# A state-space scan's 128x128 products split into 64x64 products on quadrants of the array

## The chip, the cores and the metric

The kernel runs on one core of a Trainium2 chip. The metric is device time in microseconds (us), from the launch to the end of one execution; smaller is better. A core has a matrix engine (TensorE, PE in the profile, with its weight loads as PEld), a vector engine (VectorE, DVE), an engine for activations (ScalarE, ACT), a general engine (GpSimd, POOL) and one that issues transfers (SyncE, SP). Each runs its own queue in order and waits for the others through semaphores. Matrix products are written to PSUM, a small memory of banks; everything else lives in SBUF, 128 partitions wide.

## The reference

The program is a Perceiver of two layers. 16 batches of 64 latent tokens of width 128 (1,024 tokens, `X`) attend to 1,601 context tokens per batch with 16 heads; each layer adds the attention, then a sequence model, then a feed-forward. The second layer's sequence model is a state-space scan with four heads of width 64 and state 64:

```python
dt = softplus(x @ dt_w.T + dt_b)
Bm = (x @ B_w.T).reshape(B_, L, NHEADS, D_STATE)
Cm = (x @ C_w.T).reshape(B_, L, NHEADS, D_STATE)
A = -exp(A_log)
def step(h, inp):
    x_t, dt_t, B_t, C_t = inp
    A_bar = exp(A[None, :] * dt_t)[..., None, None]
    h = A_bar * h + dt_t[..., None, None] * B_t[:, :, None, :] * x_t[..., None]
    y_t = einsum('bhpn,bhn->bhp', h, C_t) + D[None, :, None] * x_t
    return h, y_t
```

The scan starts from zero for each batch and runs over its 64 tokens. Written without a loop, y at token t is the sum over tokens s up to t of (C_t . B_s) times exp of the sum of A dt over the tokens after s up to t, times dt_s x_s, plus D x_t. That is a 64x64 lower-triangular matrix per batch and head. No token of one batch touches another batch.

## The kernel before

The attention is one long stream of steps. A step n of a group (a batch and half of its heads, `step`) issues one scores matmul of 512 columns (line 697, tile `s`) and, about 21 steps later, four averages of 129 columns (line 760, tile `av`). ScalarE evicts the scores (line 710) and takes their exponential (line 748); VectorE keeps the running maximum (line 705) and subtracts it (line 747). Three PSUM banks hold scores, two hold averages, and three more, with the tag `tp`, are shared by all other products.

Everything else is fed into this stream. `run` holds a list of generators, `between`, for the sequence models and feed-forwards of finished token groups. At each step it has a budget; the generator of the first entry is advanced, and the number that it yields, a guess at VectorE's work, is taken off the budget. A yielded tuple instead postpones the next advance by so many steps. The instructions that come out are then placed by a planner with estimates of its own, under order constraints set by `behind`, so neighbouring instructions can change places. For the second layer the entries are, in turn, `scan1` and `ffn` for chunks 0-1, 2-3, 4-5, then 6, then 7 (a chunk, c, is 128 tokens: two batches). The last entries, for chunk 7, run after the attention has ended, with nothing beside them but dummy products (`fill`, line 130).

In `scan1` a chunk goes through these products, each over both batches of the chunk at once, 128 tokens by 128 tokens:

- Line 1272 (`af`): on VectorE, the mask `after` (token later than another, same batch) times A dt, for four heads, 128x512.
- Line 1299 (`gr`): B transposed times C, per head, with 64 rows (the state) by 128 tokens, 128 columns. Two PSUM banks per chunk, one for each half of the state rows. Line 1301 (`gm`) copies it to SBUF times the mask `upto`.
- Line 1307 (`seg`): `af` times `upto`, per head, gives the sums of A dt in the exponent; line 1310 takes the exponential back into `af`.
- Line 1320: `gm` times `af`.
- Line 1326 (`sy`): the result times dt x (`xd`, line 1286 on GpSimd), 128 rows by 128 tokens, 64 columns per head; line 1329 adds it to D x.

The two masks are zero wherever the tokens are of different batches; they are made by GpSimd in `setup_rest`, lines 274 to 287. For the last chunk the exponential and the product after it are done in two halves of the heads (`parts`, line 1267).

Of the kernel before, what the change touches and what calls it, by code (L numbers as in the profile page):

```python
# [36 lines left out]
AF = mybir.ActivationFunctionType  # L37
ALU = mybir.AluOpType
# [4 lines left out]
P = 128  # L43
NB, L, D = 16, 64, 128
# [29 lines left out]
CG = 2  # L74
# [5 lines left out]
class Kernel:  # L80
# [171 lines left out]
    def setup_rest(self):  # L252

        nc, a, tc = self.nc, self.a, self.tc
        self.col = self.cst([P, 44], "col")
        nc.sync.dma_start(out=self.col, in_=a["col128"])

        self.ycol = self.cst([P, 4], "ycol")
        nc.sync.dma_start(out=self.ycol, in_=a["vec256"].rearrange("(n p) -> p n", p=P))
        nc.vector.tensor_scalar_mul(self.ycol, self.ycol, 0.5)  # L260

        self.half = self.cst([P, 10], "half")
        nc.vector.tensor_scalar_mul(self.half, self.col[:, C_CW:C_CW + 10], 0.5)
        self.vecs = self.cst([P, 20], "vecs")
        nc.sync.dma_start(out=self.vecs, in_=a["vecs"].partition_broadcast(P))

        self.na0, self.na1 = self.cst([P, 2, NS], "na0"), self.cst([P, 4], "na1")
        nc.scalar.activation(self.na0, self.col[:, C_ALOG:C_ALOG + 2 * NS].rearrange("p (k s) -> p k s", k=2), AF.Exp)
        nc.vector.tensor_scalar(self.na0, self.na0, 1e-6, 1.0, ALU.max, ALU.min)
        nc.vector.tensor_scalar_mul(self.na0, self.na0, -1.0)  # L270
        nc.scalar.activation(self.na1, self.vecs[:, V_AL:V_AL + 4], AF.Exp)
        nc.vector.tensor_scalar_mul(self.na1, self.na1, -1.0)

        self.upto = self.cst([P, P], "upto")
        nc.gpsimd.memset(self.upto, 1.0)
        nc.gpsimd.affine_select(
            out=self.upto, in_=self.upto, compare_op=ALU.is_ge, fill=0.0, base=0,
            pattern=[[1, P]], channel_multiplier=-1,
        )
        nc.gpsimd.memset(self.upto[0:64, 64:128], 0.0)  # L280
        self.after = self.cst([P, P], "after")
        nc.gpsimd.memset(self.after, 1.0)
        nc.gpsimd.affine_select(
            out=self.after, in_=self.after, compare_op=ALU.is_gt, fill=0.0, base=0,
            pattern=[[-1, P]], channel_multiplier=1,
        )
        nc.gpsimd.memset(self.after[64:128, 0:64], 0.0)
        iota_i = self.cst([P, NE], "iota_i", I32)
        nc.gpsimd.iota(iota_i, pattern=[[1, NE]], base=0, channel_multiplier=0)
        self.iota = self.cst([P, NE], "iota")  # L290
        nc.vector.tensor_copy(self.iota, iota_i)
        self.iota8 = self.cst([P, NE], "iota8")
        nc.vector.tensor_scalar_add(self.iota8, self.iota, float(NE))
        yield 1.0

        self.mcol = self.cst([P, G + 1, NB], "mcol")
        with tc.tile_pool(name="msk", bufs=1) as one:
            m8 = one.tile([NB, S], U8, tag="m8", name="m8")
            nc.sync.dma_start(out=m8, in_=a["mask"])
            mf = one.tile([NB, S], F32, tag="mf", name="mf")  # L300
            nc.vector.tensor_scalar(mf, m8, -1.0, -NEG, ALU.add, ALU.mult)
            t = self.tp("mskT")
            for g in range(G + 1):
                n = P if g < G else REM
                nc.tensor.transpose(t[:n, g * NB:(g + 1) * NB], mf[:, g * P:g * P + n], self.ident[:NB, :NB])
            me = t[:, (G + 1) * NB:(G + 2) * NB]
            nc.tensor.transpose(me, mf[:, SK:SK + 1].to_broadcast([NB, P]), self.ident[:NB, :NB])
            nc.vector.tensor_copy(self.mcol[:, :G, :].rearrange("p g b -> p (g b)"), t[:, :G * NB])
            nc.vector.tensor_copy(self.mcol[:REM, G, :], t[:REM, G * NB:(G + 1) * NB])
            nc.vector.memset(self.mcol[REM:, G, :], 0.0)  # L310
            self.mex = self.cst([P, NB], "mex")
            nc.vector.tensor_copy(self.mex, me)
        yield 2.0
        yield from self.quant_weights()
# [843 lines left out]
    def scan1(self, c0, CG):  # L1158
        nc, tc, a = self.nc, self.tc, self.a
        X = self.X[:, c0:c0 + CG, :]  # L1160
        TG, BG = CG * P, 2 * CG
        NH, HD = 4, 64
        last = c0 + CG == C and CG == 1
        with tc.tile_pool(name="sd1", bufs=1) as one, tc.tile_pool(name="sd2", bufs=CG) as work:
# [24 lines left out]
            if last:  # L1189
                cv = self.tp("cv")  # L1190
                for k in range(2):
                    o = cv[:, k * TG:(k + 1) * TG]
                    nc.tensor.matmul(o, self.wcb[:, k * P:(k + 1) * P], self.one, start=(k == 0), stop=False)
                for k in range(2):
                    o = cv[:, k * TG:(k + 1) * TG]
                    for i in range(4):
                        mm = nc.tensor.matmul(o, self.wcv[k][:, i, :], padded[:, :, i:i + L], start=False, stop=(k == 1 and i == 3))  # L1197
                self.fill(3, mm)
            else:
                t = self.tp("xz")  # L1200
# [6 lines left out]
                for k in range(2):  # L1207
                    o = cv[:, k * TG:(k + 1) * TG].rearrange("p (b l) -> p b l", l=L)
# [11 lines left out]
            t = self.tp("sdt")  # L1220
# [13 lines left out]
            t = self.tp("sz")  # L1234
# [19 lines left out]
            def bc(dst, m):  # L1254
                t = self.tp("sb")
                for hh in range(2):
                    for k in range(2):
                        nc.tensor.matmul(t[:, hh * TG:(hh + 1) * TG], m[:, k, hh * P:(hh + 1) * P], xc[:, k, :], start=(k == 0), stop=(k == 1))
                nc.scalar.copy(dst.rearrange("p h t -> p (h t)"), t[:, :2 * TG])

            bT, cT = t1([P, 2, TG], "bT"), t1([P, 2, TG], "cT")
# [2 lines left out]
            yield HOP1  # L1264
            nc.vector.scalar_tensor_tensor(dt, dt, 0.0, ln, ALU.max, ALU.add)
            nc.vector.tensor_tensor(adt, dt, self.row(self.na1, shape), ALU.mult)
            parts = ((0, 2), (2, NH)) if last else ((0, NH),)

            full = [P, NH, P]
            af = [work.tile(full, F32, tag="af", name=f"af{c}") for c in range(CG)]  # L1270
            for c in range(CG):
                x = nc.vector.tensor_tensor(af[c], self.row(self.after, full), self.bc(adt[:, c, :], full), ALU.mult)
            if last:
                self.later(nc.vector.scalar_tensor_tensor(*silu), x)
            bc(cT, CwT)
            yield 0.6 + 0.7 * CG

            xr, xd = t1([P, CG, NH, HD], "xr"), t1([P, CG, NH, HD], "xd")
            t = self.tp("sx")
# [11 lines left out]

            gm = [work.tile(full, F32, tag="gm", name=f"gm{c}") for c in range(CG)]
            for c in range(CG):
                tok = slice(c * P, (c + 1) * P)
                for i in range(2):
                    g = self.tp(f"gr{c}{i}")
                    part = slice(i * HD, (i + 1) * HD)
                    for k in range(2):
                        nc.tensor.matmul(g[:, k * P:(k + 1) * P], bT[part, k, tok], cT[part, k, tok], start=True, stop=True)
                    gi = gm[c].rearrange("p (k i) t -> p i k t", i=2)[:, i]  # L1300
                    nc.vector.tensor_tensor(gi, g[:, :2 * P].rearrange("p (k t) -> p k t", k=2), self.row(self.upto, [P, 2, P]), ALU.mult)
                yield 0.9
            for c in range(CG):
                for lo, hi in parts:
                    sg = self.tp(f"seg{c}")
                    for h in range(lo, hi):
                        mm = nc.tensor.matmul(sg[:, h * P:(h + 1) * P], af[c][:, h, :], self.upto, start=True, stop=True)  # L1307
                    if last and hi == NH:
                        self.fill(2, mm)
                    decay = nc.scalar.activation(af[c][:, lo:hi, :].rearrange("p h t -> p (h t)"), sg[:, lo * P:hi * P], AF.Exp)  # L1310
                yield 0.1
            for dst, i in ((zb, 2), (z, 0)):
                for k in range(2):
# [2 lines left out]
                        self.later(x, decay)  # L1316
            yield HOP1
            for c in range(CG):
                for lo, hi in parts:
                    nc.vector.tensor_tensor(gm[c][:, lo:hi, :], gm[c][:, lo:hi, :], af[c][:, lo:hi, :], ALU.mult)  # L1320
                yield 0.8
            yield HOP
            for c in range(CG):
                o = self.tp(f"sy{c}")
                for h in range(NH):
                    mm = nc.tensor.matmul(o[:, h * HD:(h + 1) * HD], gm[c][:, h, :], xd[:, c, h, :], start=True, stop=True)
                if last:
                    self.fill(5, mm)
                nc.vector.tensor_tensor(y[:, c, :], y[:, c, :], o[:, :256], ALU.add)
                yield 0.4  # L1330
# [3 lines left out]
            t = self.tp("syt")  # L1334
            for c in range(CG):
                for k in range(2):
                    mm = nc.tensor.transpose(t[:, k * TG + c * P:k * TG + (c + 1) * P], y[:, c, k * P:(k + 1) * P], self.ident)
# [3 lines left out]
            t = t[:, :2 * TG]  # L1341
# [372 lines left out]
```

## Time and profile before

| | |
|---|---|
| Median of 3 runs | 1975.37 us (1974.5 to 1977.61) |
| Profiled execution | 1973.36 us |
| Its span, first to last instruction | 1971.6 us |
| TensorE busy | 1931.2 us |
| VectorE busy | 1582.9 us |
| ScalarE busy | 1383.5 us |
| GpSimd busy | 512.3 us |
| Mean granted TensorE clock | 0.998 of full speed |

The products `gr`, `seg` and `sy` of the five scans lie at 1498 to 1512 us of the span, 1602 to 1625, 1777 to 1789, 1892 to 1899 and 1946 to 1950. Up to about 1934 the attention runs beside them.

A line of the profile names an engine, the source line, the operation, the tile written and the tiles read, a size in partitions by elements, and a count. In order of time the first two numbers are start and length in us; what stands in square brackets is how long the engine was idle before, and who ended it. Matmuls are pipelined, so the length of one includes its way through the array: the pace of a stream is read from one start to the next. The operations of float32 matmuls are recorded as two instructions each.

### The profile page before, as it was taken

Reading aid. Unit: us, or ns where it says so; the run is one execution under the profiler, and the core shown is the slowest. Engines: PE = TensorE matmul, PEld = TensorE weight load, DVE = VectorE, ACT = ScalarE, POOL = GpSimd, SP = SyncE. Lnnn points to the kernel's source line nnn. Section 1 sums busy time; section 2 is a strip of 40 time slices with the busy share of each in tenths; the row PEclk is TensorE's granted clock in tenths of the full one; section 3 lists DMA queues with packets and bytes.
Section 4 is the critical chain, followed back from the end, with each engine's and each line's share of the span. In section 5 each row is a group of like instructions: output and inputs, shape, how many; then the busy total and the mean of one; then the engine's idle time right before and its main releaser. Section 6 shows DMA issues by size and latency. Waiting matters only on the chain. (4 is left out here: it accounts for less than half of the span.)

```text
span 1971.6 us, 32642 instructions
## 1 busy us (share of the span) xinstructions
PE 1931.2 (98%) x11987; PEld 1478.8 (75%) x11987; DVE 1582.9 (80%) x3029; ACT 1383.5 (70%) x2638; POOL 512.3 (26%) x579
## 2 busy tenths in 40 slices
PE   8999999999999999999999999999999999999998
PEld 5777777677777767777777777777778777787786
DVE  6977776987878887876998878898786978778875
ACT  5888787887868878666776657776665665766651
POOL 5211122543123452121452202542110111101000
PEclk9999999999999999999999999999999999999999
DMA  6121112322122221221221112221120210201000
GB/s 184 46 68 51 39 54 77 85 67 70 35 76 85 66 77 53 67 78 59 77 82 54 41 40 64 70 58 54 49 67 1 58 37 19 59 18 37 23 1 23
DMA packets 146223, 111.86 MB, mean 57 GB/s; under 512 B 13827, under 2 KB 132367, under 8 KB 146063
## 3 DMA queue, kind: packets, MB, share of 16 engines
q1 hardware_dynamic: 145518, 109.51, 19.1%
q8 instruction: 95, 1.56, 0.3%
q14 instruction: 66, 0.53, 0.1%
q10 hardware_dynamic: 544, 0.26, 0.0%
HBM read 81.28 MB, written 27.41 MB: 55 GB/s over the span
## 5 line engine op out<-in xcount | busy, mean ns | idle before, releaser
L760 PEld LDWEIGHTS av<-kv,st 128*128 128x128 f32 x6656 | 870.0, 192 | 376.6 <-issue 357.5
L760 PE MATMUL av<-kv,st 128*128 128x129 f32 x6656 | 881.8, 275 | 4.0 <-DVE aq L769 4.0
L697 PE MATMUL s<-qT,kvT 128*128 128x512 f32 x1664 | 859.3, 599 | 7.4 <-ACT st L712 5.5
L748 ACT ACTIVATE st<-st 128x1024 f32<-128x1024 f32 (+1 forms) x448 | 444.3, 996 | 120.7 <-DVE st L747 114.1
L747 DVE TENSOR_TENSOR st<-st,mb 128x1024 f32<-128x1024 f32 (+1 forms) x448 | 503.7, 1134 | 17.9 <-PE mb L739 17.9
L710 ACT ACTIVATE st<-s,mcol 128x512 f32<-128x512 f32 x416 | 283.2, 684 | 191.3 <-DVE R L705 167.6
L712 ACT COPY st<-s 128x512 f32<-128x512 f32 x416 | 240.0, 580 | 133.6 <-DVE R L707 121.4
L705 DVE SCALAR_TENSOR_TENSOR R<-s,mcol,R 128x512 f32<-128x512 f32 x352 | 262.2, 745 | 43.9 <-PE s L697 42.4
L707 DVE TENSOR_TENSOR R<-s,R 128x512 f32<-128x512 f32 x352 | 241.0, 685 | 61.9 <-PE s L697 59.8
L697 PEld LDWEIGHTS s<-qT,kvT 128*128 128x128 f32 x1664 | 254.5, 192 | 21.6 <-ACT st L712 10.3
L613 POOL TENSOR_TENSOR kv<-kv,vec 128x384 f32<-128x384 f32 (+1 forms) x128 | 131.8, 1050 | 149.5 <-PE kt L672 36.2
L809 POOL TENSOR_TENSOR aq<-aq,rd 128x512 f32<-128x512 f32 x63 | 74.4, 1181 | 341.4 <-DVE rd L808 329.9
L913 POOL TENSOR_TENSOR db<-sc_u,bb 128x512 f32<-128x512 f32 x64 | 83.7, 1310 | 120.2 <-DVE h L924 63.4
L930 POOL TENSOR_TENSOR sc_y<-sc_y,h 128x512 f32<-128x512 f32 x60 | 81.9, 1365 | 116.6 <-DVE h L929 100.0
L924 DVE TENSOR_TENSOR_SCAN h<-da,db 128x512 f32<-128x512 f32 x64 | 91.8, 1434 | 0.5 <-ACT da L912 0.5
L663 ACT ACTIVATE kv<-kv,coff,crstd 128x128 f32<-128x128 f32 x182 | 76.2, 490 | 6.0 <-POOL coff L660 6.0
L769 DVE SCALAR_TENSOR_TENSOR aq<-xeb,ee,av 128x129 f32<-128x129 f32 x252 | 76.3, 341 | 0.0
L654 ACT ACTIVATE scr<-kv,cmean 128x128 f32<-128x128 f32 x182 | 72.7, 399 | 2.8 <-DVE cmean L650 0.6
L135 POOL TENSOR_TENSOR crstd<-cvar,neghalf 128x13 f32<-128x13 f32 x14 | 34.2, 2440 | 138.1 <-DVE cvar L658 137.7
L490 PE MATMUL q<-xnT,wqk 128*128 128x128 f32 x512 | 68.1, 276 | 0.8 <-ACT qT L499 0.8
L490 PEld LDWEIGHTS q<-xnT,wqk 128*128 128x128 f32 x512 | 62.7, 192 | 4.1 <-issue 1.6
L681 ACT ACTIVATE kvT<-kvT,vcol 128x768 f32<-128x768 f32 (+1 forms) x62 | 58.2, 959 | 3.9 <-DMA xhT<-kvT 3.9
(419 smaller groups left out, 1896.7 us busy)
## 6 DMA issues: line engine op xcount, KB each, us to landing
bb<-bcd SPq DMA_DIRECT2D x64, 256.0 KB, 4.4
xh<-kv SPq DMA_DIRECT2D x16, 832.0 KB, 4.7
kv<-xh SPq DMA_DIRECT2D x16, 832.0 KB, 5.6
kvT<-xhT SPq DMA_DIRECT2D x16, 800.0 KB, 4.6
xhT<-kvT SPq DMA_DIRECT2D x15, 800.0 KB, 3.4
kv<-in_ctx_dram SPq DMA_DIRECT2D x15, 768.0 KB, 5.6
ew<-in_e1T_dram SPq DMA_DIRECT2D x36, 64.0 KB, 1.9
ew<-in_e3T_dram SPq DMA_DIRECT2D x36, 64.0 KB, 2.0
```

The costliest lines, as they stand in the source:

```text
L490: nc.tensor.matmul(t[:, k * P:(k + 1) * P], self.wqk[:, g * 4 + k, :], xnT, start=True, stop=True)
L613: nc.gpsimd.tensor_tensor(kv[:, lo:hi, :D], kv[:, lo:hi, :D], self.row(self.vec[:, w1, :], [P, hi - lo, D]), ALU.mult)
L697: mm = nc.tensor.matmul(s, self.kv_of[lay, b][1][:, i * P:(i + 1) * P], q, start=True, stop=True)
L705: mx = nc.vector.scalar_tensor_tensor(R, s, mc, last, ALU.add, ALU.max)
L707: mx = nc.vector.tensor_tensor(R, s, last, ALU.max)
L710: ev = nc.scalar.activation(st, s, AF.Identity, bias=mc)
L712: ev = nc.scalar.copy(st, s)
L747: nc.vector.tensor_tensor(st, st, self.row(mb, [P, n, NQ]), ALU.subtract)
L748: nc.scalar.activation(st, st, AF.Exp)
L760: nc.tensor.matmul(grp["av", j][:, k, :], st, self.kv_of[lay, b][0][:, i, :], start=(i == 0 and k == 0), stop=(i == NT - 1 and k == 1))
L913: nc.gpsimd.tensor_tensor(db, u, self.row(bb[:, 0, s % 2, :], both), ALU.mult)
L924: nc.vector.tensor_tensor_scan(flat(h), flat(da), flat(db), 0.0, ALU.mult, ALU.add)
```

## The change

The masks `upto` and `after` become 64 columns wide, one 64x64 triangle for each half of the partitions. `af`, `gm` and the exponential become 64 tokens wide per head in place of 128, so a chunk's vectors have 256 elements per partition in place of 512, with batch 0 on partitions 0 to 63 and batch 1 on 64 to 127. Each of the products `gr`, `seg` and `sy` of a head becomes two products, one per batch, with a 64x64 stationary operand and 64 columns. `seg` and `sy` read and write the same half of the partitions; `gr` reads the half that holds the head's state and writes the half of the batch. `gr` now takes both PSUM banks of a chunk before its first product. The last chunk is no longer done in two halves. The yielded guesses go down by 0.3 in three places per chunk.

```diff
-        self.upto = self.cst([P, P], "upto")
...
-        nc.gpsimd.memset(self.after[64:128, 0:64], 0.0)
+        self.upto, self.after = self.cst([P, L], "upto"), self.cst([P, L], "after")
+        for t, op, sign in ((self.upto, ALU.is_ge, 1), (self.after, ALU.is_gt, -1)):
+            nc.gpsimd.memset(t, 1.0)
+            for b in range(2):
+                half = t[b * L:(b + 1) * L]
+                nc.gpsimd.affine_select(
+                    out=half, in_=half, compare_op=op, fill=0.0, base=0,
+                    pattern=[[sign, L]], channel_multiplier=-sign,
+                )
...
-            parts = ((0, 2), (2, NH)) if last else ((0, NH),)
-            full = [P, NH, P]
+            full = [P, NH, L]
+            both = [slice(b * L, (b + 1) * L) for b in range(2)]
...
-            yield 0.6 + 0.7 * CG
+            yield 0.6 + 0.4 * CG
...
             gm = [work.tile(full, F32, tag="gm", name=f"gm{c}") for c in range(CG)]
             for c in range(CG):
-                tok = slice(c * P, (c + 1) * P)
+                gs = [self.tp(f"gr{c}{i}") for i in range(2)]
+                for k in range(2):
+                    for i in range(2):
+                        part = slice(i * HD, (i + 1) * HD)
+                        for b in range(2):
+                            tok = slice(c * P + b * L, c * P + (b + 1) * L)
+                            nc.tensor.matmul(gs[i][both[b], k * L:(k + 1) * L], bT[part, k, tok], cT[part, k, tok], start=True, stop=True)
                 for i in range(2):
-                    g = self.tp(f"gr{c}{i}")
-                    part = slice(i * HD, (i + 1) * HD)
-                    for k in range(2):
-                        nc.tensor.matmul(g[:, k * P:(k + 1) * P], bT[part, k, tok], cT[part, k, tok], start=True, stop=True)
                     gi = gm[c].rearrange("p (k i) t -> p i k t", i=2)[:, i]
-                    nc.vector.tensor_tensor(gi, g[:, :2 * P].rearrange("p (k t) -> p k t", k=2), self.row(self.upto, [P, 2, P]), ALU.mult)
-                yield 0.9
+                    nc.vector.tensor_tensor(gi, gs[i][:, :2 * L].rearrange("p (k t) -> p k t", k=2), self.row(self.upto, [P, 2, L]), ALU.mult)
+                yield 0.6
             for c in range(CG):
-                for lo, hi in parts:
-                    sg = self.tp(f"seg{c}")
-                    for h in range(lo, hi):
-                        mm = nc.tensor.matmul(sg[:, h * P:(h + 1) * P], af[c][:, h, :], self.upto, start=True, stop=True)
-                    if last and hi == NH:
-                        self.fill(2, mm)
-                    decay = nc.scalar.activation(af[c][:, lo:hi, :].rearrange("p h t -> p (h t)"), sg[:, lo * P:hi * P], AF.Exp)
+                sg = self.tp(f"seg{c}")
+                for h in range(NH):
+                    for b in both:
+                        mm = nc.tensor.matmul(sg[b, h * L:(h + 1) * L], af[c][b, h, :], self.upto[b], start=True, stop=True)
+                if last:
+                    self.fill(2, mm)
+                decay = nc.scalar.activation(af[c].rearrange("p h t -> p (h t)"), sg[:, :NH * L], AF.Exp)
                 yield 0.1
...
             for c in range(CG):
-                for lo, hi in parts:
-                    nc.vector.tensor_tensor(gm[c][:, lo:hi, :], gm[c][:, lo:hi, :], af[c][:, lo:hi, :], ALU.mult)
-                yield 0.8
+                nc.vector.tensor_tensor(gm[c], gm[c], af[c], ALU.mult)
+                yield 0.5
...
                 for h in range(NH):
-                    mm = nc.tensor.matmul(o[:, h * HD:(h + 1) * HD], gm[c][:, h, :], xd[:, c, h, :], start=True, stop=True)
+                    for b in both:
+                        mm = nc.tensor.matmul(o[b, h * HD:(h + 1) * HD], gm[c][b, h, :], xd[b, c, h, :], start=True, stop=True)
```

More of the change, by code (lines that the diff above doesn't have):

```diff
@@ L272, in setup_rest @@
         nc.vector.tensor_scalar_mul(self.na1, self.na1, -1.0)
-        self.upto = self.cst([P, P], "upto")
[L275 to L286, printed above, removed]
-        nc.gpsimd.memset(self.after[64:128, 0:64], 0.0)
+        self.upto, self.after = self.cst([P, L], "upto"), self.cst([P, L], "after")
[7 more added lines that the diff above has]
+                )
         iota_i = self.cst([P, NE], "iota_i", I32)
```

## The prediction

> **What bounds the kernel now.** I read the busy times first, then what TensorE waited for, then the order of time around the changed lines, then the end.
>
> Busy times of the page:
>
> ```profile
> PE 1931.2 (98%) x11987; PEld 1478.8 (75%) x11987; DVE 1582.9 (80%) x3029; ACT 1383.5 (70%) x2638; POOL 512.3 (26%) x579
> ```
>
> TensorE (PE) is taken nearly all the time, VectorE has a fifth of the span free. A busy PE alone proves little, so I take the distance from one group of matmuls to the next. One instruction in the records is one pass; a matmul of float32 shows as two. Order of time on PE, the first two-chunk scan:
>
> ```profile
> 1495.01 1.05 PE L760 MATMUL av<-kv,st 128*128 128x129 f32 x8
> 1495.90 1.02 PE L697 MATMUL s<-qT,kvT 128*128 128x512 f32 x2
> 1496.76 1.05 PE L760 MATMUL av<-kv,st 128*128 128x129 f32 x8
> 1497.74 1.94 PE L1299 MATMUL gr<-sd_cT,sd_bT 64*128 64x128 f32 x16
> 1499.61 1.16 PE L1307 MATMUL seg<-upto,af 128*128 128x128 f32 x8
> 1500.60 1.02 PE L697 MATMUL s<-qT,kvT 128*128 128x512 f32 x2
> ...
> 1510.29 1.90 PE L1326 MATMUL sy<-sd_xd,gm 128*128 128x64 f32 x16
> 1512.02 1.11 PE L490 MATMUL q<-xnT,wqk 128*128 128x128 f32 x8
> ```
>
> Two passes of 512 columns take 1496.76 - 1495.90 = 0.86 us, 0.84 ns per column; eight passes of 129 columns take 0.89, 0.111 each. The groups stand shoulder to shoulder: the two attention lines run at this pace through all of the second layer. So PE sets the time there, and a nanosecond taken from its queue is a nanosecond of the kernel. Of waits by VectorE on PE between 1480 and 1936 us, only one on this change's lines is large:
>
> ```profile
> PE gr L1299 <- DVE gm L1301: 1.8, 1, 1.8
> ```
>
> Order of time on PE in the second two-chunk scan, with the row of the stretch 1605 to 1610 (busy time of each engine, then the granted clock):
>
> ```profile
> 1602.29 1.32 PE L1299 MATMUL gr<-sd_cT,sd_bT 64*128 64x128 f32 x12
> 1603.54 1.12 PE L697 MATMUL s<-qT,kvT 128*128 128x512 f32 x2
> 1606.51 0.77 PE L1299 MATMUL gr<-sd_cT,sd_bT 64*128 64x128 f32 x4 [1.84 <-DVE gm L1301]
> 1607.20 2.08 PE L1307 MATMUL seg<-upto,af 128*128 128x128 f32 x8
> 1609.07 1.72 PE L760 MATMUL av<-kv,st 128*128 128x129 f32 x8
> 1610.63 0.60 PE L820 MATMUL at<-ident,aq 128*128 128x128 f32 x4
> ...
> 1605.00:1610.00 5.00, 3.49 (x17) 3.32 (x18) 2.59 (x7) 2.27 (x5) 0.57 (x1) 0.70 0.03 12
> ```
>
> The last four gr passes wait 1.84 us for a PSUM bank that gm must empty, and VectorE is late with it because two af products of 128x512 come first. After the stall the clock is 0.70 in these 5 us: eight seg passes take 1.87 us for 0.90 (what eight take at 1611.06 to 1611.96), eight av passes 1.56 for 0.89, four gr 0.69 for 0.42, 1.9 us more. This one wait costs 3.7 us.
>
> **The change part by part.** *Removed from PE.* A chunk (128 tokens, two batches) has 8 passes each of gr, seg and sy. Steady paces: gr 0.104 (12 passes from 1602.29 to 1603.54), seg 0.1125, sy 0.108 (16 from 1510.29 to 1512.02). That is 0.83 + 0.90 + 0.87 = 2.60 us a chunk. Seven of the eight chunks lie under the attention's stream: 18.2 us of PE.
>
> *Added to PE.* 16 passes each, 64x64 stationary and 64 columns. The trace has no such tile, but a near one, the first layer's 64 queries by 64 keys per head, 32 rows by 64 columns of the array, four row bands in turn:
>
> ```profile
> 487.75 1.05 PE L760 MATMUL av<-kv,st 128*128 128x129 f32 x8
> 488.73 0.69 PE L998 MATMUL ms<-mo_kT,mo_q 32*64 32x64 f32 x32
> 489.36 1.12 PE L697 MATMUL s<-qT,kvT 128*128 128x512 f32 x2
> ```
>
> 32 passes in 0.63 us, 0.0197 each. Alone, 64 columns would take 64 x 0.84 = 0.054. So tiles of different bands do overlap, about 2.7 times. Bounds for a 64x64 pass: 0.0197 and 0.054. gr goes round all four quadrants: I take 0.0197, 0.315 us a chunk. seg and sy go between two quadrants on the diagonal: two at once at best give 0.027; I take 0.030, 0.48 each. Sum 1.275 a chunk, 8.9 us for seven: 9.3 us less. All three at 0.0197 would be 6.6 us (11.6 less); all at 0.054 would be 18.1 (0.1 less).
>
> Here two rules speak against the change. The Trainium skill, TensorEngine Tiling (Array Packing), section Restrictions and Gotchas, says that different row tiles can't use the same PSUM bank at once. seg and sy write both quadrants of a chunk into one bank, on its upper and lower 64 partitions. By this rule they would run one after the other: 0.864 in place of 0.48, twice, seven times, 5.4 us of the gain gone. But L998 does the same: heads 0 and 1 sit on rows 0 to 31 and 32 to 63 and write the two halves of one bank, at 0.0197. I go by the row. The same page, section Tiling Modes, says that a change of tiling mode drains the array, without a price. The trace has the price: the eight av passes ahead of L998 last 0.98 us where 0.89 is usual, and so do those ahead of gr at 1496.76. 0.09 us for each entry. gr pays it already; seg and sy, whole-array passes until now, will, in about eight places: +0.7. The way out lies within the 0.63. Net on PE: -8.6 us.
>
> *The bank wait.* The new gr loop asks for two banks of a chunk at once, from three. The second chunk again can't begin until gm has emptied one. Before it, VectorE now has af at 128x256 (about 0.42 by the same-shaped product L1329, against 0.78 mean and 1.0 in this place) and gm at 128x128 (0.28 by L836, against 0.42). The built order puts a scores pair and three av passes between the two chunks' gr in the second scan, none in the first, one pair in the third. With shorter gr passes PE arrives sooner, too. I take half of the 3.7 us back: -2.0, between 0 and -4 (the 0.26 of the first scan with it).
>
> *VectorE and ScalarE under the stream.* Per chunk af gains 0.36, gm 2 x 0.14, gm times af 0.27 (0.69 to 0.42), the exponential 0.21 (0.595 to 0.384). Nothing of it is on the path where PE is, beyond what is counted; at the end it is.
>
> *The last chunk, alone.* Order of time:
>
> ```profile
> 1945.77 0.69 DVE L1272 TENSOR_TENSOR af<-after,sd_adt 128x512 f32<-128x512 f32 x1
> 1947.60 0.83 ACT L1310 ACTIVATE af<-seg 128x256 f32<-128x256 f32 x2 [1.71 <-PE seg L1307]
> 1948.02 0.87 DVE L1320 TENSOR_TENSOR gm<-gm,af 128x256 f32<-128x256 f32 x2 [0.55 <-ACT af L1310]
> 1948.71 1.00 PE L1326 MATMUL sy<-sd_xd,gm 128*128 128x64 f32 x8
> 1949.82 0.42 DVE L1329 TENSOR_TENSOR sd_y<-sd_y,sy 128x256 f32<-128x256 f32 x1 [0.93 <-PE sy L1326]
> ```
>
> Today seg starts at 1946.85, released by the silu product behind af. af becomes 0.27 shorter: seg from 1946.58. Sixteen passes to the last start 0.45, 0.2 to its end, 0.14 to the exponential: 1947.4, 0.38 long. Then one gm times af, 1947.8 to 1948.25; sy from 1948.3, done 1948.98; the add at 1949.1. Giving up the two overlapped halves is in this. -0.7; with passes of 0.054 it is 0, at 0.0197 -0.9.
>
> *No price.* The masks are made by GpSimd at 24 to 27 us, in instructions of 0.15 to 0.29 us (six before, six after), over 1,400 us ahead of their first use. SP's order changes in two places: two weight loads of the third scan go ahead of a kvT load. They wait for the preceding feed-forward's buffers, and that load is issued some 48 steps (over 80 us) before its use; without this cover the delay would fall on the s line, whole.
>
> *Moved.* The smaller yields (0.3 less in three places per chunk) bring each later stage of the layer forward by some steps of 2 us, and the instructions of feed-forward and scan meet other steps of the attention. PE's waits on all engines in this stretch are 4.1 us; I put new ones at 0, between -1 and +4.
>
> Sum: -8.6 - 2.0 - 0.7 = -11.3 us. The profiled execution took 1973.36 (span 1971.6, 1.8 around it): 1962.1. The median of the runs, 1975.37, is 2.0 above it: 1964.1.
>
> **Rivals.** *No overlap in 64x64 quadrants.* For: two passes of one matmul share a tile and follow each other, and the diagonal has two tiles where L998 has four. Against: its 0.0197. Then -0.1 + 0.7 - 2.0, end 0: 1974.0, no change to be measured. *Everything at L998's pace, the stall gone.* -11.6 + 0.7 - 4.0 - 0.9: 1959.6. For: af is halved where it was late. *Slower: the bank wait becomes the rule.* Both banks of the second chunk hang on gm, in all three two-chunk scans, behind VectorE's backlog. One stall costs its length s and some 1.9 us of clock. It eats the 9.3 of PE and end (8.6 + 0.7) and the 4.0 saved when 3(s + 1.9) is over 13.3, s over 2.5 us. At s = 5, 20.7: 1982.8. Against: each af is half as long, and s was 0.26, 1.84 and none before.
>
> **How the numbers follow.** The forecast 0.62 (1962 to 1968 by its bounds); all at L998's pace 0.13; no overlap 0.13; slower 0.07; the forecast with new waits of some 6 us, about 1970, 0.05. Less than 0.2%, 4 us, is about what a measurement can't tell from no change. Faster: 0.62 + 0.13 + 0.04 = 0.79; same 0.14; slower 0.07. The range, 1959 to 1972, takes in the forecast, the fast rival and the one with new waits and leaves out the other two, 0.2.
>
> **What would show it.** Right: 32 gr passes under 0.8 us, 32 seg or sy passes near 1 us; av groups of 0.98 ahead of seg and sy; the wait of gr on gm under 1 us, no stretch at clock 0.70; from af of the last chunk to the add after sy 3.3 us in place of 4.05. Wrong: 64x64 passes near 0.05 each, seg slower than gr by more than twice, or PE waiting for gm, for the exponential or for hb in each scan.

## The result, and the profile after

The changed kernel takes 1965.72 us in the median of seven runs (1964.7 to 1968.43), beside 1974.5 for the kernel before in the same comparison (1971.53 to 1977.61). The two medians lie 8.8 us apart; the ratio of the runs, 0.9964 with an interval of 0.9954 to 0.9974, puts the gain at 7.1 us, between 5.1 and 9.1, and is what is used below. The forecast was 1964.1, 11.3 us less than before. The direction and the range hold, the size of the gain does not quite, and its parts turn out quite different from the sum that was made.

The profiled execution spans 1966.4 us. Busy times of its page:

```profile
PE 1925.9 (98%) x12179; PEld 1471.0 (75%) x12179; DVE 1576.1 (80%) x3028; ACT 1380.4 (70%) x2637; POOL 511.4 (26%) x579
```

TensorE is still taken 98% of the span, with 192 passes more in the records and 5.3 us less busy time. Order of time on PE in the second two-chunk scan, where the wait for a bank was:

```profile
1595.06 1.05 PE L755 MATMUL av<-kv,st 128*128 128x129 f32 x8
1596.04 0.46 PE L1296 MATMUL gr<-sd_cT,sd_bT 64*64 64x64 f32 x16
1596.43 1.13 PE L692 MATMUL s<-qT,kvT 128*128 128x512 f32 x2
...
1598.65 0.65 PE L1296 MATMUL gr<-sd_cT,sd_bT 64*64 64x64 f32 x16 [0.43 <-DVE gm L1299]
...
1600.09 1.15 PE L1305 MATMUL seg<-upto,af 64*64 64x64 f32 x32
1601.17 1.13 PE L692 MATMUL s<-qT,kvT 128*128 128x512 f32 x2
1602.13 1.05 PE L755 MATMUL av<-kv,st 128*128 128x129 f32 x8
...
1603.89 1.05 PE L755 MATMUL av<-kv,st 128*128 128x129 f32 x8
1604.87 1.15 PE L1324 MATMUL sy<-sd_xd,gm 64*64 64x64 f32 x32
```

The wait of gr on gm has gone from 1.84 to 0.43 us. 16 passes of gr take 1596.43 - 1596.04 = 0.39 us, 32 passes of seg take 1601.17 - 1600.09 = 1.08. The averages ahead of a visit to the quadrants (1603.89 to 1604.87) take 0.98 us where 0.89 is usual, and the scores behind one (1601.17 to 1602.13) 0.96 where 0.86 is usual: both ways cost 0.1.

Among the waits of PE between 1480 and 1932 us, the largest first, a new one leads:

```profile
PE syt L1335 <- DVE sd_y L162: 2.0, 1, 2.0
...
PE gr L1296 <- DVE gm L1299: 0.4, 1, 0.4
```

It lies in the third scan, at the transpose of the scan's normalized output. Order of time on PE there, with the row of the stretch 1785 to 1790 (busy time of PE, PEld, DVE, ACT and POOL, then the granted clock):

```profile
1781.59 1.05 PE L755 MATMUL av<-kv,st 128*128 128x129 f32 x8
1784.63 0.73 PE L1335 MATMUL syt<-ident,sd_y 128*128 128x128 f32 x4 [1.99 <-DVE sd_y L162]
1785.20 1.38 PE L692 MATMUL s<-qT,kvT 128*128 128x512 f32 x2
1786.38 1.93 PE L755 MATMUL av<-kv,st 128*128 128x129 f32 x8
...
1785.00:1790.00 5.00, 5.00 (x20) 3.77 (x20) 3.03 (x6) 2.64 (x4) 0.00 (x0) 0.66 0.57 174
```

After the 1.99 us wait the clock is 0.66 over 5 us: a scores pair takes 1.18 us and eight averages 1.72. With the 0.85 of the at group that follows, for the usual 0.44, these three groups take 1.6 us more than they do at the full clock (0.32, 0.83 and 0.41), and the stall costs some 3.6 in all. What VectorE waited for, order of time on POOL and DVE:

```profile
1779.41 2.09 POOL L608 TENSOR_TENSOR kv<-kv,vec 128x512 f32<-128x512 f32 x2 [2.86 <-DMA kv<-xh]
1781.58 0.19 POOL L155 TENSOR_SCALAR var<-mv 128x2 f32<-128x2 f32 x1
1781.86 0.95 POOL L608 TENSOR_TENSOR kv<-kv,vec 128x384 f32<-128x384 f32 x1
1782.76 0.70 POOL L135 TENSOR_TENSOR rstd<-var,neghalf 128x2 f32<-128x2 f32 x1
1783.50 1.31 DVE L162 TENSOR_SCALAR sd_y<-sd_y,mv,rstd 128x256 f32<-128x256 f32 x2 [3.87 <-POOL rstd L135]
```

GpSimd computes the scan's 1/sigma in two small instructions (0.19 and 0.70 us). They stand in its queue among the products that scale the attention's context (L608), which had themselves just waited 2.86 us for a transfer. What the first of them reads (`mv`, line 145) was done on VectorE at 1778.58, 3.0 us before it started at 1781.58. The scan now comes to this point earlier, and the small instructions meet that queue.

The last chunk, which runs alone, from af to the add behind sy (DVE and PE in order of time):

```profile
1941.28 0.42 DVE L1268 TENSOR_TENSOR af<-after,sd_adt 128x256 f32<-128x256 f32 x1
1942.09 0.68 PE L1305 MATMUL seg<-upto,af 64*64 64x64 f32 x16 [0.19 <-DVE sd_z L1270]
1942.70 1.13 PE L130 MATMUL fill<-wvo,ident 128*128 128x256 f32 x4
...
1944.60 0.42 DVE L1327 TENSOR_TENSOR sd_y<-sd_y,sy 128x256 f32<-128x256 f32 x1 [0.94 <-PE sy L1324]
```

1944.60 - 1941.28 = 3.32 us, where it was 4.05.

### The profile page after: what moved, and what is told of

Read it like the earlier page. It is cut to its first block, busy times and chain, and to the rows that moved or that the text cites. A ratio compares the mean times of both kernels' runs of the same rounds, so it can differ in the third digit from the quotient of the medians.

```text
span 1966.4 us, 33027 instructions
## 1 busy us (share of the span) xinstructions
PE 1925.9 (98%) x12179; PEld 1471.0 (75%) x12179; DVE 1576.1 (80%) x3028; ACT 1380.4 (70%) x2637; POOL 511.4 (26%) x579
## 3 DMA queue, kind: packets, MB, share of 16 engines
q8 instruction: 96, 1.57, 0.3%
## 5 line engine op out<-in xcount | busy, mean ns | idle before, releaser
L608 POOL TENSOR_TENSOR kv<-kv,vec 128x384 f32<-128x384 f32 (+1 forms) x128 | 131.6, 1048 | 144.2 <-PE kt L667 35.9
```

The lines of the kernel that those rows point to most:

```text
L608: nc.gpsimd.tensor_tensor(kv[:, lo:hi, :D], kv[:, lo:hi, :D], self.row(self.vec[:, w1, :], [P, hi - lo, D]), ALU.mult)
```

## The experiments

To compare profiles below the scatter of whole executions I also use a distance between landmarks: from the first scores pass of the second layer's first scan to the last scores pass of the attention, the same 364 passes in every kernel. I call it the stream. It is 430.3 us before and 424.6 after. The part ahead of it, where no code on the path differs, came out between 0.8 us shorter and 2.9 us longer than before, from one profile to another.

### The changed products in the old order: e1_old_yields

The change has two halves: the products, and the guesses that the scan yields, which set when its stages run. This kernel keeps the new products and takes the old guesses.

```diff
-            yield 0.6 + 0.4 * CG
+            yield 0.6 + 0.7 * CG
...
-                yield 0.6
+                yield 0.9
...
-                yield 0.5
+                yield 0.8
```

> The 64x64 products and half-wide vectors, with the yields of the kernel before, so that the stages stand where they stood. Theory: the products give their part wherever they stand: about 7.5 to 8.5 us of PE and 0.7 us at the end; the GpSimd wait ahead of syt in the third scan (3.9 us with its loss of clock) is not there, and the bank wait in the second scan comes back, but under 1 us since af is half as long. 1963 to 1966 against 1974.5, ratio 0.9940 to 0.9960. Rival: the new places brought much of the gain: ratio 0.9975 or more.

Measured: 1964.81 us, ratio 0.9960 (0.9946 to 0.9975); stream 422.8. The wait for the bank is there again and the wait for GpSimd is gone; waits of PE in the same stretch:

```profile
PE gr L1296 <- DVE gm L1299: 1.4, 1, 1.4
```

The wait for the bank was expected to come back under 1 us and is 1.4. So the new places are not needed for the gain, and halving the vectors does not by itself take the bank wait away. It is a matter of the order: the changed kernel lost one stall and found another.

### The new order with the old products: e2_new_yields

The other half alone: the kernel before, with the three guesses lowered as in the change.

> The kernel before with nothing changed but the three yields, so that its 128x128 products stand about where the changed kernel's stand. Theory: places only trade one wait for another: within 3 us of the kernel before, ratio 0.9985 to 1.0015; whichever wait is left shows with clock 0.7 behind it. Rival: the places brought the gain: ratio 0.9975 or less.

Measured: 1971.32 us, ratio 0.9994 (0.9985 to 1.0002), no difference that can be told; stream 428.1, 2.2 us less than before. Waits of PE:

```profile
PE syt L1337 <- DVE sd_y L162: 1.3, 1, 1.3
...
PE gr L1299 <- DVE gm L1301: 0.4, 1, 0.4
```

The 128x128 products at the new places have the changed kernel's pair: 0.4 us on the bank, and a wait for sd_y in the third scan, 1.3 us where the changed kernel has 2.0. The low clock that was expected behind it isn't there: 1.00 from 1785 to 1790 us. Neither the end of the old stall nor the new one comes from the quadrants.

### Two steps later: e4_later_sy and e4_again

If the new wait comes from the scan being too early in GpSimd's queue, putting sy of the third scan (chunks 4 and 5) two attention steps later should remove it, with the products untouched.

```diff
-            yield HOP
+            yield HOP4 if c0 == 4 else HOP
```

> The changed kernel, with sy of the third scan put off by two steps, so that its layer norm's small GpSimd work stands behind all of the context's products and PE meets syt later. Theory: the 3.9 us of that wait and its clock go and nothing takes their place: about 11 us under the kernel before, ratio 0.9935 to 0.9952. Rival: the wait moves to another product or stage: ratio 0.9960 to 0.9968, as the changed kernel.

Measured: 1963.72 us, ratio 0.9953 (0.9939 to 0.9968); stream 420.0, 4.6 us less than the changed kernel. To tell the size from the scatter it ran again, beside the changed kernel and the two kernels that follow.

> The changed kernel with sy of the third scan put off, once more in more rounds: 0.9940 to 0.9958, stream 420 us. It has to stand below the changed kernel of the same call by 3 to 5 us for the GpSimd wait to be worth what the trace says; if the two are within 1.5 us, the wait is paid elsewhere.

> The changed kernel, unchanged, on the same chip: 0.9958 to 0.9970, stream 424.5 us, with the wait ahead of syt.

Measured: 1963.74 us (0.9951, 0.9938 to 0.9963) against 1966.8 for the changed kernel unedited (0.9969, 0.9957 to 0.9980). All five runs of the one (1961.87 to 1964.75) lie below all six of the other (1965.88 to 1969.09): 3.1 us between the medians. Order of time on PE and POOL with sy two steps later:

```profile
1785.52 0.60 PE L716 MATMUL tm<-ident,R 128*128 128x128 f32 x4
1785.96 0.60 PE L1335 MATMUL syt<-ident,sd_y 128*128 128x128 f32 x4
```
```profile
1778.42 3.87 POOL L608 TENSOR_TENSOR kv<-kv,vec 128x512 f32<-128x512 f32 x4 [2.78 <-DMA kv<-xh]
...
1782.65 0.70 POOL L135 TENSOR_TENSOR rstd<-var,neghalf 128x2 f32<-128x2 f32 x1
```

syt now waits for nothing, although 1/sigma is no earlier on GpSimd: TensorE has other work to do until 1785.96. The context products still wait for their transfer, but TensorE does not wait for them.

The second profile of the changed kernel shows something else. Its wait is the same, and its clock is not (waits of PE; row of the stretch 1785 to 1790):

```profile
PE syt L1335 <- DVE sd_y L162: 2.0, 1, 2.0
```
```profile
1785.00:1790.00 5.00, 5.00 (x33) 3.86 (x32) 4.00 (x10) 3.22 (x5) 0.00 (x0) 1.00 0.51 167
```

Clock 1.00, and a stream of 423.0 in place of 424.6. The 1.6 us between the two profiles is what the low clock costs; it doesn't always follow the wait.

The traces hold the stretches of low clock themselves. Each in the middle of a kernel is 3.41 us long, at half speed, and starts on a grid of that step that runs through the whole execution. Two steps of this grid in the first profile of the changed kernel, then two in the second (busy time of PE is the first number behind the comma, the clock the one behind POOL):

```profile
1782.32:1785.73 3.41, 1.42 (x9) 0.90 (x9) 2.19 (x5) 0.00 (x0) 2.02 (x3) 1.00 0.04 9
1785.73:1789.14 3.41, 3.41 (x15) 2.90 (x14) 2.33 (x5) 1.95 (x3) 0.00 (x0) 0.50 0.78 242
```
```profile
1781.95:1785.36 3.41, 1.61 (x8) 1.04 (x9) 2.70 (x7) 0.29 (x1) 1.51 (x2) 1.00 0.14 25
1785.36:1788.77 3.41, 3.41 (x27) 2.93 (x27) 2.58 (x4) 2.59 (x5) 0.00 (x0) 1.00 0.65 230
```

In the first the whole wait lies in one step, which leaves TensorE 1.42 us of work in it; in the second 0.18 us of the wait fall into the step ahead, and 1.61 us of work are left. In the ten traces of this case, between 60 and 1940 us, half clock follows the four steps with the least work, 1.42, 1.51, 1.55 and 1.57 us (the last is the stall of the kernel before), and none of the others, of which this 1.61 is the lowest. Near the start and the end of a kernel, some steps with up to 1.97 us are followed by half clock and some with 1.69 and more are not, so the busy time of the records is not the whole rule; and no kernel was made to move a wait across the grid.

### The old products without either stall: e6_before_later_sy

The kernel before with the lowered guesses and the same two steps: the order of the previous kernel, with 128x128 products. It splits the gain in two: before to this is places, this to the previous is products.

> The kernel before with the new yields and with sy of the third scan put off by two steps: the 128x128 products without either of the large waits. Theory: the wait of 3.7 us ahead of gr and the one of syt (1.3 us and its clock in the run with new yields alone) are both gone, so the stream from the second layer's first scan to its end is 426 to 427 us against 430.2, and the time 0.9975 to 0.9990 of the kernel before. The 64x64 products without these waits (stream 420.0) are then 6.5 to 7 us better, and 0.7 more at the end. Rival: what the waits cost is less than they seem, and this is no faster than the run with new yields alone, 0.9994, stream 428.

Measured: 1969.77 us in the median of 21 runs, ratio 0.9980 (0.9974 to 0.9987); stream 425.6. Two of PE's waits that are left:

```profile
PE gr L1299 <- DVE gm L1301: 0.4, 1, 0.4
PE ft L1441 <- DVE hb L1380: 0.3, 1, 0.3
```

The second of them in the kernel before:

```profile
PE ft L1441 <- DVE hb L1380: 1.2, 2, 0.9
```

So 3.7 us (3.9 by the ratio, 2.6 to 5.1) of the kernel before are removed by an order of work alone, with no product changed. The products then bring 1969.77 - 1963.74 = 6.0 us, of which the stream shows 5.2 (425.6 to 420.4; 6.5 to 7 were expected) and the end of the last chunk 0.7. By tile, from one start to the next, the stream of this kernel against that with the new products (e4_again):

| | passes | us | passes | us | difference |
|---|---|---|---|---|---|
| gr | 56 | 5.48 | 112 | 2.90 | -2.58 |
| seg | 56 | 6.35 | 112 | 3.94 | -2.41 |
| sy | 56 | 6.03 | 112 | 3.85 | -2.19 |
| av and s, same passes | | 320.1 | | 321.9 | +1.8 |

A wait counts with the pass ahead of it, so the 0.4 us ahead of gr stand in the last row, in both kernels. The rest of that row is the way into and out of the quadrants: TensorE goes there 14 times, before only gr did, 6 times. With the first profile of the same kernel (e4_later_sy) it is +1.5.

### The pace of quadrants by itself: m1_pace

At the end of the kernel two series of dummy products (`fill`), whose results nobody reads, were replaced by sets of 16 products on the array's parts, 32 passes with 64 columns each, between whole-array products `sep` of 2 passes by 256 columns. The rest is the changed kernel.

```diff
-            self.fill(10, mm)
+            self.pace(0, mm)
...
+            for i in range(16):
+                b = (lo, hi)[i % 2]
+                made.append(nc.tensor.matmul(*tile(t[0], b, b, i // 2 % 4), start=True, stop=True))
+            sep()
+            t = new("b")
+            for i in range(16):
+                b = (lo, hi)[i % 2]
+                made.append(nc.tensor.matmul(*tile(t[i % 2], b, b, i // 2 % 4), start=True, stop=True))
+            sep()
...
```

> The changed kernel with its last two rows of dummy products replaced by 16 products each of seven forms, 64 columns each, between whole-array dummy products; no time is asked. Per pass of 32. a, the diagonal in one bank as in seg and sy: 0.034. b, the diagonal with a bank for each row half: 0.034 if the number of tiles sets the pace, near 0.027 if the shared bank costs. c, one quadrant only: 0.054 if a lone tile is bound by its columns. d, four quadrants in gr's order: 0.024 to 0.026; e, four quadrants with the row half changing each time: the same if order is nothing, near 0.020 if gr's order costs. f, four bands of 32 rows as in the first layer: 0.020. g, one row half and two column halves: 0.034 if column halves overlap, 0.054 if they don't.

Order of time on PE:

```profile
1948.86 1.15 PE L152 MATMUL pacea<-wvo,ident 64*64 64x64 f32 x32
1949.94 0.70 PE L142 MATMUL sep<-wvo,ident 128*128 128x256 f32 x2
1950.57 1.15 PE L157 MATMUL paceb<-wvo,ident 64*64 64x64 f32 x32
1951.65 0.70 PE L142 MATMUL sep<-wvo,ident 128*128 128x256 f32 x2
1952.28 2.08 PE L161 MATMUL pacec<-wvo,ident 64*64 64x64 f32 x32
1954.28 0.70 PE L142 MATMUL sep<-wvo,ident 128*128 128x256 f32 x2
...
1956.77 0.59 PE L142 MATMUL sep<-wvo,ident 128*128 128x256 f32 x2
1957.30 0.69 PE L166 MATMUL paced<-wvo,ident 64*64 64x64 f32 x32
1957.92 0.70 PE L142 MATMUL sep<-wvo,ident 128*128 128x256 f32 x2
...
1961.06 1.15 PE L181 MATMUL paceg<-wvo,ident 64*64 64x64 f32 x32
1962.14 0.70 PE L142 MATMUL sep<-wvo,ident 128*128 128x256 f32 x2
```

From the start of each set to the start of `sep` behind it:

| set | us | per pass | per pass without 0.15 |
|---|---|---|---|
| a: two diagonal quadrants, one bank | 1.08 | 0.0338 | 0.029 |
| b: the same, a bank each | 1.08 | 0.0338 | 0.029 |
| c: one quadrant alone | 2.00 | 0.0625 | 0.058 |
| d: four quadrants, in gr's order | 0.62 | 0.0194 | 0.015 |
| e: four, the row half changing each time | 0.63 | 0.0197 | 0.015 |
| f: four bands of 32 rows | 0.62 | 0.0194 | 0.015 |
| g: one row half, both column halves | 1.08 | 0.0338 | 0.029 |

The last column takes off what a group costs whatever its length. That is seen where the same products come in groups of 16 and of 32 passes. On four quadrants gr takes 0.39 us for 16 (above) and 0.63 for 32 (1595.04 to 1595.67 in the kernel that follows), so 16 more take 0.24, 0.015 each, and 0.15 is fixed. On the diagonal seg takes 0.61 for 16 (1942.09 to 1942.70 in the last chunk) and 1.08 for 32, so 16 more take 0.47, 0.029 each, and 0.14 is fixed. The starts of the single records say the same: on any one part, passes begin 0.058 us apart in every set, only the second comes 0.05 later, and `sep` starts some 0.1 later than a further pass would.

The number of different parts of the array that are in use sets the pace: with two in turn a pass takes half as long as with one, with four a quarter. In which bank they write, in which order they come and whether they differ in rows or in columns does not matter. Two of the expectations were missed, c (0.0625 for 0.054) and d (0.0194 for 0.024 to 0.026); the latter was the 0.39 us of gr's short groups, with the fixed part in it. And `sep`, 512 columns, 0.43 us at the pace of the attention's scores, takes 0.53 with a set behind it only (1956.77 to 1957.30), 0.54 with one ahead only (1954.28 to 1954.82), and 0.63 with one on each side: 0.1 us on the way in and 0.1 on the way out. With the 0.15 inside, a visit costs some 0.35 us besides its passes.

### Fewer visits, shared banks: e5_shared_banks

A version made from these findings. Since a bank may be shared, gr of both chunks goes into the same two banks and seg and sy of both into one each, so that no chunk should wait for a bank of the other. The products of seg move ahead of gm, and sy of the third scan stays two steps later.

```diff
+            gs = [self.tp(f"gr{i}") for i in range(2)]
             for c in range(CG):
-                gs = [self.tp(f"gr{c}{i}") for i in range(2)]
...
-                            nc.tensor.matmul(gs[i][both[b], k * L:(k + 1) * L], bT[part, k, tok], cT[part, k, tok], start=True, stop=True)
+                            nc.tensor.matmul(gs[i][both[b], (2 * c + k) * L:(2 * c + k + 1) * L], bT[part, k, tok], cT[part, k, tok], start=True, stop=True)
...
+            sg = self.tp("seg")
...
+            o = self.tp("sy")
```

> The changed kernel with sy of the third scan put off and the products of both chunks of a scan put into common banks: two for gr, one for seg, one for sy, gr of both chunks first and then seg. Theory: gr no longer waits for gm (0.43 us), and three visits of 64x64 mode fewer in the stream at 0.2 us each: 1 us under the same kernel with banks of its own, stream 419.0, ratio 0.9938 to 0.9955. Rival: seg now stands ahead of gm and PE waits for af, or DVE reads the banks later: stream over 420.

Measured: 1962.41 us, ratio 0.9944 (0.9932 to 0.9957), the lowest median of all: 4.4 us under the changed kernel in the same comparison, and 1.3 under e4_again, which the runs (1961.13 to 1962.87 against 1961.87 to 1964.75) don't separate. Its stream is 419.3 against 420.4, and most of the difference lies in gr: 2.16 us in place of 2.90. It goes to the quadrants 11 times in place of 14; three visits at 0.35 us are 1.05. Order of time on PE, second scan:

```profile
1595.04 0.69 PE L1296 MATMUL gr<-sd_cT,sd_bT 64*64 64x64 f32 x32
1595.67 1.12 PE L692 MATMUL s<-qT,kvT 128*128 128x512 f32 x2
...
1598.14 1.15 PE L1301 MATMUL seg<-upto,af 64*64 64x64 f32 x32 [0.68 <-DVE gm L1307]
```

gr of both chunks goes in one visit; a wait of 0.68 on gm remains, now at seg. What ties seg to gm there was not traced.

## Why the prediction was right, and where it was not

The gain with its parts, as the runs give them, beside the sum of the forecast:

| step | forecast | shown by | us |
|---|---|---|---|
| PE's passes and the visits | -8.6 | e6 to e4, stream | -5.2 to -5.7 |
| the bank wait | -2.0 | 3.7 less the 0.4 that is left | -3.3 |
| last chunk | -0.7 | 4.05 to 3.32 | -0.7 |
| moved stages, hb in the second feed-forward | 0 | before to e6, rest of 4.7 | -1.0 to -1.4 |
| moved stages, sd_y behind GpSimd | 0 | after to e4, stream | +2.6 to +4.6 |

The rows add up to between -8.5 and -5.6; measured -7.1. The two rows of the moved stages and the first are where the forecast failed; that they partly cancel within the total is luck. The hb row is what the other rows leave over; the trace shows 0.9 us of it as a wait.

*Removed from PE* was right: 17.9 us for seven chunks (5.48 + 6.35 + 6.03) where 18.2 was put.

*Added to PE* was too low: 10.7 us (2.90 + 3.94 + 3.85) for 8.9. That does not come from the paces. The 0.030 of seg and sy was right (0.029), and the 0.0197 of gr was too high (0.015): at these the passes alone come to 8.2 us (28 rounds of four for gr and 56 rounds of two each for seg and sy, 0.0585 us a round). What is missing is the fixed part of a visit, 14 times 0.15 = 2.1 us; the rest, some 0.4, are slower gr groups in the first and second scan. The 0.63 us of L998 has this part in it, too. Divided by 32 passes it looks like pace, 0.0197 for 0.015, and an overlap of 2.7 times where it is four. For seg and sy it is 1.1 us.

*The rule on banks.* The Trainium skill (TensorEngine Tiling (Array Packing), section Restrictions and Gotchas) would have put 5.4 us on it. I set it aside for L998, and the sets a and b settle it: 1.08 us with one bank, 1.08 with two, when the quadrants write different halves of the partitions. The 1.08 us are therefore the time of two quadrants, not a penalty for the bank.

*The change of mode* was priced at a quarter: 0.1 us going in, as read, but 0.15 inside the group and 0.1 coming out. Outside the groups, 8 visits more make 1.6 us (measured 1.5 to 1.8) for 0.7. The step that failed is "The way out lies within the 0.63", and with it the reading of the 0.63 as passes alone. The line shown in the forecast said otherwise: the scores pair behind L998 is 1.12 us long, and those behind whole-array groups 1.02. I had read the length of the group ahead and not that of the group behind.

*The bank wait* went almost whole, where I took half; that was the upper part of my bounds. But the reason given, halved af and gm, is not what did most of it. With the old products and only new places it goes too (e2_new_yields), with the new products and old places it stays at 1.4 us (e1_old_yields). What removes it is where the scan's stages meet the attention's steps.

*Moved.* Zero was wrong in both directions, at +4 the bound I gave just about held. The earlier scan cured one wait for hb (0.9 us in the kernel before) and made one for sd_y. I named VectorE, ScalarE and SP as what hides moved work, and never followed the layer norm through GpSimd, which is only 26% busy but takes its queue in order: two instructions of together 0.9 us came behind context products that a transfer held up.

*One stall costs its length and some 1.9 us of clock* was read from one case and used as a rule. It holds in the profile before (1.84 us, clock 0.70) and the first one after (1.99, 0.66), not in the second one after (1.98, 1.00). The Trainium skill (TensorE: Matmul & The Clock Gate, section What's actually happening) says that the clock is either whole or half, decided over windows of 3413 ns that run on by themselves. The traces agree: the stretch at 0.50 is 3.41 us long and lies on a grid of that step, so it loses 1.7 us rather than the 1.9 read, and the place of the wait on the grid fits whether it comes. The page asks for a whole idle window, though; here a step with 1.57 us of work in 3.41 was enough.

*The rivals.* No overlap is out (0.029 and 0.015 against 0.058). All at L998's pace is out for seg and sy. Slower by the bank is out. The forecast with new waits, given 0.05 and some 6 us, has the right mechanism at half the size.

## What to carry to other kernels

Price work on parts of the array by how many different parts it uses in turn, and add the fixed cost of each visit, here some 0.35 us; collect visits rather than spread them. Take a pace from two groups of different length, since a single group has the fixed part in it, and read the group behind as well as the one ahead. When an edit changes the guesses by which work is interleaved, run the guesses alone and the edit alone: here 3.7 us lay in the order and 6.0 in the products, and the change brought the second while trading one stall for another. Follow a moved stage through every queue that it uses, the idle ones too, since a small instruction waits behind whatever is ahead of it.

## What the hardware showed that was not expected

- A pass of 64 columns comes every 0.058 us on one quadrant, every 0.029 on two and every 0.015 on four: the parts overlap fully. Two run at the same pace on the diagonal and side by side on the same rows (1.08 us for 32 passes), so column halves overlap as row halves do.
- A group on quadrants also costs some 0.15 us whatever its length (0.39 us for 16 passes of gr, 0.63 for 32).
- A bank shared by two quadrants that write different partitions costs nothing (1.08 and 1.08).
- Going out of the quadrants costs as much as going in, 0.1 us each.
- The same idle time of TensorE, 2.0 us at the same place of the same kernel, was once followed by 3.41 us at half clock and once by none; the two streams differ by 1.6 us. The first left 1.42 us of work in its step of the clock's grid, the second 1.61.
